# Three places where VectorE stands still in a stack of selective scans: copies of xc moved, an output addition moved, 664 dt x B products given to VectorE

## The chip, the cores and the metric

One core of one Trainium2 chip runs the whole program. The metric is the time of one execution on the device in microseconds, as a median of repeated runs. The profile is of one more execution, and its span runs from the first instruction to the last.

Five engines work side by side, each through its own queue in order: PE (TensorE, matrix products into PSUM), DVE (VectorE), ACT (ScalarE), POOL (GpSimd) and SP (SyncE, which here issues the DMAs).

## The reference, cut to what matters

The input is 8 images of 192 channels and 56 x 56 points. Four layers follow, each a residual on a group norm:

```python
x = x + _L0_conv_ref(_gn(x), ...)
x = x + _L1_conv_ref(_gn(x), ...)
x = x + _L2_conv_ref(_gn(x), ...)
x = x + _L3_conv_ref(_gn(x), ...)
```

Layer 0 applies filters made from each point to 5 x 5 patches; layers 1 to 3 are Mamba layers with an inner width of 512, 384 and 384. The heart of these is the selective scan over the points of an image, with 16 states for each inner channel:

```python
xc = silu(causal_conv(xi) + conv_b)
dbl = xc @ x_proj_W.T
dt = softplus(dt_low_rank @ dt_proj_W.T + dt_proj_b)
h = h * exp(dt[..., None] * A) + (dt * xc)[..., None] * B[:, None, :]
y = einsum('nds,ns->nd', h, C) + xc * D
out = (y * silu(z)) @ out_proj_W.T
```

`dbl` holds the low-rank dt, B and C of 16 each. Layer 1 puts a layer norm before and after, and the three slices of 64 channels share their weights.

## The kernel before, in words

Each image is cut into 7 chunks of T = 448 points; 56 chunks a layer. A **job** is one chunk in layers 2 and 3 (the dense layers, `nd` = 3 groups of 128 inner channels) and one chunk and slice in layer 1 (`nd` = 4, 168 jobs). A job has `nd` x 4 **units**: one group j of 128 channels and one q of four groups of 4 states, so 16 units in layer 1 and 12 in the dense layers; 2688 + 672 + 672 = 4032 in all. A unit lies on 128 partitions (32 channels x 4 states) and has four rows (the 4 times 32 channels), taken in two halves h of two rows.

What a unit k needs, by function, line and engine:

- `decays` (L721, ACT): the exponentials of dt x A for one half, two of them, into a PSUM bank of that half.
- `inputs_lo` (L738, DVE): dt x xc times B for the low half. B was spread over the partitions by a small matmul, `spread_b` (L715, PE), into a PSUM pool with one buffer, `banks.b`. The one for unit k+2 can therefore only begin when DVE has read that of k+1.
- `inputs_hi` (L734, POOL): the same product for the high half, with B out of `rows[0, q]` in SBUF, which a DMA loads (`row_in`, L620).
- `inputs_begin` (L729, ACT): the state at the chunk's start into column 0. `keep` (L746, ACT) saves the last column.
- `scan` (L742, DVE): the recurrence, one instruction for each half.
- `readout` (L751, POOL, twice): the states times C, in place; so it has to wait for `keep` of the same unit. `reduce` (L757, L760, PE) sums over the states, and `gated` (L776, DVE) multiplies a finished group with silu(z).

dt and dt x xc come to the units through memory: `softplus` (L634, ACT) makes dt, `x_again` (L638, PE) copies xc into PSUM, `dtx` (L641, DVE) multiplies the two, `store` sends the group to DRAM (`ops`), and `load_ops` reads it back spread over the partitions (`rep`, two buffers for each half). `load_when_free` issues these loads from SP's queue.

**The order is written out by hand** in `ssm_layer`. The body of unit k issues, in this order: `gated` and `reduce(k-3)`; the plan's place 2m; `scan(k, 0)`; `decays(k+1, 0)`; `inputs_begin(k+3)`; `inputs_hi(k+2)`; two `readout(k-2)`; `inputs_lo(k+1)`; `spread_b(k+2)`; the plan's place 2m+1; `scan(k, 1)`; `keep(k)`; `decays(k+1, 1)`, where m is the unit's number in its job. Idle slots on PE get filler matmuls (`nothing`, L766).

The next job's preparation, and the end of the job before (its output projection and the addition to the stream), are laid into the 2 x `per_job` **places** of a job by `places`. Preparation consists of `Step`s: matmuls, the operation that empties the PSUM bank (`rest`), a cost that spreads the steps over a stretch of places, and `left`: how many emptying operations may still be outstanding when the step begins. `Steps.run` first empties down to `left`, then issues the matmuls. The matmuls' pool `mm` has two buffers. `bounds` says where the stretches begin: the silu block stands at place 8 (dense), 10 (layer 1, first slice) or 6, the softplus block 6 (dense) or 8 places later. A step with `closes` ends its place.

```python
def run(self, steps):
    for step in steps:
        self.flush(step.left)
        ...
            step.matmuls()
            self.pending.append(step.rest)
```

A **block** is where ACT changes its table of functions and back: `silu` (xc at L587, silu(z) of the running job at L568, reload at L560) and `softplus` (L634 and its reload). During a block ACT makes no decays.

In a dense job, `meanwhile` (right behind the silu block) holds the two `out_proj` steps of the job before (L1107, PE) with their additions `add` (L1113, DVE); `xproj` (L592, PE) follows, and then `left_of_b`, `delta` and the row loads. Before the change xproj's step has `left` 1, so that the first addition is issued at place 9, ahead of `scan(k, 1)`.

## Time and profile before

| what | value |
|---|---|
| median of three runs | 26,491.58 us (26,490.21 to 26,491.7) |
| the profiled execution's own time | 26,518.46 us |
| its span | 26,516.6 us |
| mean granted clock of PE | 0.835 |
| POOL busy | 24,242.3 us, 91% of the span |
| DVE busy | 22,849.2 us, 86% |
| PE busy (matmuls) | 22,170.8 us, 84% |
| ACT busy | 17,021.6 us, 64% |

By layer, inside three windows of the trace (layers 1, 2 and 3 without their ends):

| window, us | length | PE | DVE | ACT | POOL | granted clock |
|---|---|---|---|---|---|---|
| 1760 to 17925 | 16165 | 13067 | 14039 | 10852 | 15378 | 0.80 |
| 18240 to 22300 | 4060 | 3519 | 3546 | 2822 | 3824 | 0.87 |
| 22460 to 26400 | 3940 | 3493 | 3421 | 2770 | 3789 | 0.89 |

How to read the profile's lines. A line of the groups gives line, engine, operation, output <- inputs by the program's names with partitions x elements, and the number of instructions; behind the first bar the total busy time and the mean nanoseconds of one; behind the second the idle time of the engine just before them, and what ended most of it. A line of the waits gives who waited <- for whom, then total us, number of waits and the longest. A line of the timeline gives start, length, engine, line, operation and number of equal instructions in a row, and in brackets the idle time ahead and who ended it. Who ended a wait is inferred from semaphores; an engine that isn't the bottleneck may be idle at no cost.

### The profile page before, as it was taken

The page shows a single profiled execution, that of the slowest core. Times are in us where ns is not written, and L with a number is a line of the kernel's source. Part 1 is how long each engine was busy: PE and PEld are TensorE (multiplying, and loading weights), DVE is VectorE, ACT ScalarE, POOL GpSimd, SP SyncE. Part 2 cuts the span into 40 slices and gives each one's busy share as a digit, 9 for nine tenths or more (in the row PEclk, how much of TensorE's full clock was granted, in tenths as well). Part 3 has the DMA queues.
Part 4 walks back from the last instruction along what each step waited for, and adds up shares of the span by engine and source line. Part 5 has one row for each costly group of instructions (what it writes and reads, how often), then busy time and mean ns, then how long its engine had stood idle before and what let it go on. Part 6 is the DMA issues. An engine that isn't in the chain of part 4 may idle for free. (4 is left out here: it accounts for less than half of the span.)

```text
span 26516.6 us, 248987 instructions
## 1 busy us (share of the span) xinstructions
PE 22170.8 (84%) x74628; PEld 7074.0 (27%) x74628; DVE 22849.2 (86%) x17677; ACT 17021.6 (64%) x32354; POOL 24242.3 (91%) x12820
## 2 busy tenths in 40 slices
PE   9988888888888888888878888888888888888888
PEld 3322222222222222222222222222333332333332
DVE  8878888888888888888888888887888887888888
ACT  1146666666666666666666666665666666777776
POOL 4469999999999999999999999998999998999999
PEclk9987878887778787787778877878888888888888
DMA  4433333333333333333333333333344443444443
GB/s 107 110 103 121 119 118 121 119 120 120 119 118 120 120 119 118 120 121 120 117 121 118 121 116 122 119 119 107 131 134 133 134 134 120 134 134 136 140 136 123
DMA packets 1249495, 3236.48 MB, mean 122 GB/s; under 512 B 170924, under 2 KB 510916, under 8 KB 1248008
## 3 DMA queue, kind: packets, MB, share of 16 engines
q1 hardware_dynamic: 1245336, 3219.49, 37.1%
q8 instruction: 585, 9.58, 0.1%
q14 instruction: 774, 6.34, 0.1%
q10 hardware_dynamic: 2800, 1.06, 0.0%
HBM read 2502.68 MB, written 555.55 MB: 115 GB/s over the span
## 5 line engine op out<-in xcount | busy, mean ns | idle before, releaser
L742 DVE TENSOR_TENSOR_SCAN uhg<-da,uhg 128x898 f32<-128x898 f32 x8064 | 16063.3, 2013 | 1003.2 <-ACT da L721 991.9
L751 POOL TENSOR_TENSOR uhg<-uhg,rows 128x896 f32<-128x896 f32 x8064 | 15387.2, 1930 | 809.0 <-ACT carry L746 769.7
L721 ACT ACTIVATE da<-rep,k 128x448 f32<-128x448 f32 x16128 | 10262.0, 636 | 1843.9 <-DVE uhg L742 1531.9
L734 POOL TENSOR_TENSOR uhg<-rep,rows 128x896 f32<-128x896 f32 x4032 | 8407.6, 2085 | 592.2 <-DMA rep<-ops 554.0
L738 DVE TENSOR_TENSOR uhg<-rep,b 128x896 f32<-128x896 f32 x4032 | 4296.4, 1066 | 923.9 <-PE b L715 873.4
L760 PE MATMUL y<-uhg,k 128*32 128x448 f32 x32256 | 4946.3, 658 | 124.0 <-POOL uhg L751 120.6
L746 ACT COPY carry<-uhg 128x4 f32<-128x4 f32 x4032 | 787.6, 195 | 4268.1 <-DVE uhg L742 4259.3
L715 PE MATMUL b<-k,k 96*128 96x448 bf16 x4032 | 1603.6, 398 | 1903.1 <-DVE uhg L738 1895.9
L766 PE MATMUL y<-w_d,k 128*128 128x448 f32 (+1 forms) x5908 | 3015.2, 608 | 0.0
L757 PE MATMUL y<-xc,w_d 128*128 128x448 f32 x2016 | 1411.4, 793 | 835.8 <-DVE zs L776 833.5
L1008 PE MATMUL mm<-xs,k 128*128 128x448 f32 x2688 | 1345.1, 628 | 571.4 <-ACT da L721 413.1
L766 PEld LDWEIGHTS y<-w_d,k 128*128 128x128 f32 x5908 | 1174.3, 220 | 1867.8 <-issue 1841.5
L626 PE MATMUL mm<-dbl,w_dt 36*128 36x448 f32 (+1 forms) x2016 | 1580.7, 897 | 36.1 <-ACT k L608 35.5
L760 PEld LDWEIGHTS y<-uhg,k 128*32 128x32 f32 x32256 | 749.9, 116 | 3182.6 <-issue 1554.8
L1060 PE MATMUL mm<-v,w_in 96*128 96x448 f32 x2688 | 1416.4, 658 | 152.0 <-ACT zs L668 97.7
L431 POOL TENSOR_TENSOR x<-x,one 96x448 f32<-96x448 f32 x560 | 633.2, 1135 | 648.8 <-DVE one L423 631.3
L641 DVE TENSOR_TENSOR dt<-dt,mm 128x448 f32<-128x448 f32 x1008 | 609.1, 618 | 644.5 <-PE mm L638 469.5
L715 PEld LDWEIGHTS <-k 96*128 96x128 bf16 x4032 | 414.7, 103 | 2741.1 <-issue 1641.0
L631 ACT ACTIVATE dt<-mm,k 128x448 f32<-128x448 f32 x1008 | 637.2, 632 | 771.8 <-PE mm L626 761.2
L423 DVE TENSOR_TENSOR prod<-mm,shifted 128x448 f32<-128x448 f32 x1680 | 932.3, 609 | 188.1 <-PE mm L411 167.6
L1087 PE MATMUL mm<-xin,w_conv 128*128 128x448 f32 x2688 | 1076.1, 543 | 0.0
L603 PE MATMUL mm<-dbl,k 16*16 16x448 f32 x1120 | 735.1, 747 | 273.6 <-ACT dbl L596 273.6
(134 smaller groups left out, 20183.0 us busy)
## 6 DMA issues: line engine op xcount, KB each, us to landing
rep<-ops SPq DMA_DIRECT2D x4032, 448.0 KB, 4.7
rows<-bc SPq DMA_DIRECT2D x2240, 224.0 KB, 4.9
ops<-dt SPq DMA_DIRECT2D x1008, 448.0 KB, 2.8
shifted<-xpad SPq DMA_DIRECT2D x672, 179.0 KB, 4.6
xg<-stream SPq DMA_DIRECT2D x168, 336.0 KB, 3.5
xr<-stream SPq DMA_DIRECT2D x168, 336.0 KB, 4.7
stream<-xr SPq DMA_DIRECT2D x112, 336.0 KB, 3.2
xs<-xg SPq DMA_DIRECT2D x224, 112.0 KB, 2.3
```

The costliest lines, as they stand in the source:

```text
L626: nc.tensor.matmul(u.dps[j][:, :T], lhsT=w.dtw[:, j * 128 : (j + 1) * 128], rhs=u.dbl[:nk, :], start=True, stop=True)
L715: nc.tensor.matmul(brow[k][:, :T], lhsT=pick_b[:, q, :], rhs=us[i].parts, start=True, stop=True)
L721: nc.scalar.activation(t[:, 64 + 449 * r : 512 + 449 * r], reps[k // NQ][h][:, r, 0, :], AF.Exp, scale=w.neg_a[:, j * NR + 2 * h + r, q : ...
L734: nc.gpsimd.tensor_mul(uhg[k][:, 2:4, 1:], reps[k // NQ][1][:, :, 1, :], b)
L738: nc.vector.tensor_mul(uhg[k][:, 0:2, 1:], reps[k // NQ][0][:, :, 1, :], b)
L742: nc.vector.tensor_tensor_scan(v, banks.da[h][:, 63:961], v, 0.0, ALU.mult, ALU.add)
L751: nc.gpsimd.tensor_mul(v, v, us[i].rows[1, q].unsqueeze(1).to_broadcast([128, 2, T]))
L757: nc.tensor.matmul(ys[k // NQ][:, :T], lhsT=w.dd[:, j, :], rhs=us[i].xc[:, j, :], start=True, stop=False)
L760: nc.tensor.matmul(y[32 * r : 32 * r + 32, :T], lhsT=fold, rhs=uhg[k][:, r, 1:], start=False, stop=(q == NQ - 1))
L766: nc.tensor.matmul(ys[k // NQ][:, : nd * 112], lhsT=zeros, rhs=w.dd.rearrange("p j e -> p (j e)")[:, : nd * 112], start=False, stop=False,)
L1008: nc.tensor.matmul(pm[:, :T], lhsT=w.inconv[:, k, j * 128 : (j + 1) * 128], rhs=ck.xs[:, i, 2 - 2 * k : 2 - 2 * k + T], start=(k == 0), st ...
L1060: nc.tensor.matmul(pm[:, :T], lhsT=w.inw[:, k, m * 128 : (m + 1) * 128], rhs=ck.v[:, k, :], start=(k == 0), stop=(k == NCT - 1),)
```

## The change

Three things change, all in the order of the work. First, the copies of xc for groups 0 and 1 (`x_again`) are issued at the same place as the softplus block, ahead of `scan(k, 0)`, and not one place later behind `spread_b`; the first `store` step no longer lets one operation be outstanding, so that `dtx(0)` and `dtx(1)` are both issued at place softplus + 2. In the dense jobs `dtx(1)` was one place later. Second, in the dense jobs xproj's step no longer empties anything first: the first output addition is issued at place 10, behind `scan(k, 1)`, by an empty step of cost 3.5 that stands where a pause of that cost stood. Third, a set `by_vector` holds the units behind the silu block and behind the softplus block of each job with a successor and, in the dense layers, the first unit of the next job: 2 x 167 in layer 1 and 3 x 55 in each dense layer, 664 of 4032. For these, `inputs_hi` does nothing and `inputs_lo` makes both halves on DVE, B coming out of PSUM both times. `bounds` and the call of `places` are rewritten so that stretches need not adjoin.

```diff
-        stores[1].closes = True
...
-            + [settle()], [Step(None, silu, 0, 0.3, block=True), *meanwhile] + [Step(xproj, xproj_out, 1, nd)] * (nd == 3),
-            [Step(xproj, xproj_out, 0, nd)] * (nd == 4) + [pause(1.0 if nd == 4 else 3.5)]
+            + [settle()], [Step(None, silu, 0, 0.3, block=True), *meanwhile] + [Step(xproj, xproj_out, 9, nd)] * (nd == 3),
+            ([Step(xproj, xproj_out, 0, nd), pause()] if nd == 4 else [Step(None, lambda: None, 2, 3.5)])
...
-            + [settle()], [Step(None, softplus, 0, 0.3, block=True)],
-            stores[:2] + [Step(None, lambda: store(0), 1)] + stores[2:3] + [Step(None, lambda: store(1), 1)]
+            + [settle()], [Step(None, softplus, 0, 0.3, block=True)] + stores[:2],
+            [Step(None, lambda: store(0), 0)] + stores[2:3] + [Step(None, lambda: store(1), 1)]
...
+        by_vector = set()
+
         def inputs_hi(k):
+            if k in by_vector:
+                return
...
         def inputs_lo(k):
             b = brow[k][:, :T].unsqueeze(1).to_broadcast([128, 2, T])
-            nc.vector.tensor_mul(uhg[k][:, 0:2, 1:], reps[k // NQ][0][:, :, 1, :], b)
+            for h in range(2 if k in by_vector else 1):
+                nc.vector.tensor_mul(uhg[k][:, 2 * h : 2 * h + 2, 1:], reps[k // NQ][h][:, :, 1, :], b)
...
-            return 0, silu, silu + 2, softplus, softplus + 1, softplus + 4, n_places
+            return (0, silu), (silu, silu + 2), (silu + 2, softplus), (softplus, softplus + 1), (softplus + 2, softplus + 4), (softplus + 4, n_places)
...
-                    plan = places(*zip((*jobs[i + 1][2](u, us[i], outs), rest + jobs[i + 1][3](u)), at, at[1:]))
+                    by_vector |= {k + at[1][0] // 2 + 1, k + at[3][0] // 2 + 1} | ({k + per_job} if nd == 3 else set())
+                    stretches = *jobs[i + 1][2](u, us[i], outs), rest + jobs[i + 1][3](u)
+                    plan = places(*((steps, *p) for steps, p in zip(stretches, at)))
```

## The prediction

> **What bounds the kernel now.** I read the engine totals first, then the costliest groups, and then, layer by layer, whom each engine waits for.

> ```profile
> PE 22170.8 (84%) x74628; PEld 7074.0 (27%) x74628; DVE 22849.2 (86%) x17677; ACT 17021.6 (64%) x32354; POOL 24242.3 (91%) x12820
> ...
> L742 DVE TENSOR_TENSOR_SCAN uhg<-da,uhg 128x898 f32<-128x898 f32 x8064 | 16063.3, 2013 | 1003.2 <-ACT da L721 991.9
> L751 POOL TENSOR_TENSOR uhg<-uhg,rows 128x896 f32<-128x896 f32 x8064 | 15387.2, 1930 | 809.0 <-ACT carry L746 769.7
> ...
> L734 POOL TENSOR_TENSOR uhg<-rep,rows 128x896 f32<-128x896 f32 x4032 | 8407.6, 2085 | 592.2 <-DMA rep<-ops 554.0
> L738 DVE TENSOR_TENSOR uhg<-rep,b 128x896 f32<-128x896 f32 x4032 | 4296.4, 1066 | 923.9 <-PE b L715 873.4
> ```

> POOL is the busiest engine, so a change that takes 664 of its products away looks like a large gain. But the right-hand columns show POOL waiting: its readouts (L751) wait for `keep`, which is one step behind DVE's scans, and its product (L734) waits for a DMA. By layer (layer 1, then 2, then 3; total us, times, longest one):

> ```profile
> POOL uhg L751 <- ACT carry L746: 746.2, 637, 3.3
> ```
> ```profile
> POOL uhg L734 <- DMA rep<-ops: 268.2, 51, 71.7
> ```
> ```profile
> POOL uhg L734 <- DMA rep<-ops: 207.7, 53, 62.9
> ```

> The reverse wait, DVE's scan for POOL, comes to almost nothing:

> ```profile
>   ACT da L721: 991.9, 820
>   POOL uhg L751: 4.6, 10
>   POOL uhg L734: 1.0, 4
> ```

> In layer 1, POOL's own pace is 5.81 us a unit (2.04 from one product's start to the next instruction, 3.77 for two readouts), 92.9 us for a job of 16 units, and a job lasts 98.0 us. So the scan chain on DVE leads, stopping at the two table blocks of each job. In layers 2 and 3, 12 x 5.81 = 69.7 us; with 196.5/50 = 3.9 and 144.8/52 = 2.8 us of wait for `rep` (the totals less the first fill, 71.7 and 62.9) that gives 73.6 and 72.5, and the jobs last 73.9 and 72.5. POOL there is full but for one wait a job, and that wait ends when the next job's data, made by DVE, ACT and PE, comes through memory. POOL is nearly tied with the chain, not ahead of it. Only PE waits for it, in layer 3 (layer 2: 16.2 us):

> ```profile
> PE y L760 <- POOL uhg L751: 58.3, 87, 0.9
> ```

> Now the two places where DVE stands still. First the silu block of a layer 3 job (start, length, instruction, in brackets the wait):

> ```profile
> 23325.17 1.28 ACT L587 ACT_TABLE_LOAD   x1
> 23325.77 1.09 DVE L738 TENSOR_TENSOR uhg<-rep,b 128x896 f32<-128x896 f32 x1
> 23327.12 0.36 PE L715 MATMUL b<-k,k 96*128 96x448 bf16 x1
> 23327.32 4.67 PE L1107 MATMUL mm<-zs,w_out 128*96 128x448 f32 x12
> ...
> 23329.78 0.62 DVE L1113 TENSOR_TENSOR xr<-xr,mm 96x448 f32<-96x448 f32 x1 [2.92 <-PE mm L1107]
> 23330.31 1.31 ACT L721 ACTIVATE da<-rep,k 128x448 f32<-128x448 f32 x2
> 23330.32 3.93 DVE L742 TENSOR_TENSOR_SCAN uhg<-da,uhg 128x898 f32<-128x898 f32 x2
> ```

> DVE waits 2.92 us for the output projection (L1107) with a scan behind it whose decays are long there. Then the softplus block of the same job, where DVE stands at both brackets:

> ```profile
> 23347.44 1.28 ACT L634 ACT_TABLE_LOAD   x1
> ...
> 23350.88 0.62 DVE L641 TENSOR_TENSOR dt<-dt,mm 128x448 f32<-128x448 f32 x1 [1.33 <-PE mm L638]
> ...
> 23352.71 2.03 DVE L742 TENSOR_TENSOR_SCAN uhg<-da,uhg 128x898 f32<-128x898 f32 x1 [1.21 <-ACT da L721]
> ...
> 23355.64 1.15 DVE L641 TENSOR_TENSOR dt<-dt,mm 128x448 f32<-128x448 f32 x2
> ```

> [...] The moved product reads one input from PSUM, so I expect no contention; L738's mean of 1066 ns beside a busy POOL agrees. [...] The trace's granted clock is 0.80, 0.87 and 0.89 in layers 1 to 3, with PE 81, 87 and 89% busy, and I come back to this in the range.

> **The change part by part.** It touches 167 jobs of layer 1 and 55 each of layers 2 and 3 (those with a predecessor).

> Products to DVE. Two a job in layer 1 and three in the dense layers: 334 + 330 = 664. POOL loses 664 x 2.04 = 1355 us. DVE gains 664 x 0.98 = 651 us (0.98 from one product's start to the next instruction). At silu, the next decays are ready 7.20 us after L587's load in layer 1 and DVE idles 3.3 to 3.9 us, so 0.98 is hidden: cost 0. At softplus they are ready 5.61 us (layer 1) and 5.24 us (dense) after L634's load, with 2.3 to 3.0 idle: hidden too, even beside both `dtx`. If decays came earlier, each would cost up to 0.98. The first unit of a dense job has no such stall: from 5 us behind softplus to the end of the job DVE runs without a break, so 0.98 x 110 = **+108 us** on the path (between 0, where PE holds the end, and 108; I take 108). DVE's data is there: its low half starts 5.5 to 8.8 us after POOL got the same job's `rep`. POOL no longer meets the DMA at that unit: its next product comes 3.77 us later.

> The longer product holds its PSUM bank 0.98 us longer, and `spread_b(k+2)`, which writes that bank (one buffer), stands on PE ahead of the planned matmuls. At the dense silu that is L1107 and then xproj.

> Addition behind the switch. The scan no longer stands behind L1113 and its 2.92 us; it runs inside the stall. The scan after it starts 0.85 us (layer 2) and 1.21 us (layer 3) later than its decays allow now: mean 1.03 saved. Given back: L1107 starts later by 0.1 to 0.98, middle 0.54. Net -0.49 x 110 = **-54 us** (ends -0.93 and -0.05 a job). Next late is ACT's pair of decays. xproj's bank now waits for an addition of 0.62 us that comes when L1107 ends; behind it on PE stand the matmuls of place 10.

> Copies of xc beside softplus. Both `dtx` now fall into the stall. In the dense layers the second one stood ahead of a scan: 0.54 x 110 = **-59 us** (1.15 for two less the overlap: 0.54 from start to start). In layer 1 both stood there already; what goes is what the copy added to the wait, 0.09 x 167 = -15 us. The stores' DMAs on SP's queue follow `dtx`, a place earlier for the second; SP's row loads keep their order.

> PE's waits for POOL: 58.3 + 16.2 = 74.5 us at most. POOL comes 6 us a job earlier against waits of 0.9, so they go, but not all stood on the path; I take three quarters: **-56 us** (0 to -74.5).

> Layer 1 in sum: -15 as above; the few jobs in which POOL led (it waits for `keep` 637 times, not everywhere), -20 (0 to -40); `spread_b` held back at 334 units, hidden beside the table loads but for some 0.05 each, +15 (0 to 0.4 x 167 = +67). **-20 us**.

> Sum: -54 - 59 + 108 - 56 - 20 = -81 against the profiled execution's 26,518.5 (span 26,516.6): 26,437. It lay 27 above the median of the three runs, so the forecast is **26,410**. A difference of 0.2% (53 us) is about what measurement can tell from none.

> **Rivals.**
> (B) POOL leads in the dense layers. For it: 94 and 96% busy, and POOL's pace plus one wait makes up the job to 0.3 us. Against: its wait ends on the others' data. If its relief carries until DVE (64.4 and 62.8 us busy a job) or PE (64.9) stops it, I estimate half of the 6.1 us: 2.7 x 110 = -300, so 26,190.
> (C) Slower: `spread_b` behind the longer product. It stands ahead of L1107 and xproj on PE, and PE ends last in the dense stretch from silu to softplus as soon as it loses more than the 0.49 of slack that the addition's move gives. Then +0.5 x 110 + 0.4 x 167 = +122: 26,613. PE's clock works the same way: layer 1's triples of jobs last 290, 293.7 or 296.9 us[...].
> (D) Nothing: the next wait (decays behind the reload) swallows each gain, 26,490.
> (E) POOL is the bound all through: -1355, so 25,135. DVE's waits for it, 5.6 us, speak against it.

> **How the numbers follow.** Mine 0.45 (its own range 26,340 to 26,470 from the ends above), B 0.18, C 0.18, D 0.17, E 0.02. Of mine a quarter (0.11) is above 26,439, within 0.2%. Faster 0.34 + 0.18 + 0.02 = 0.54; same 0.11 + 0.17 = 0.28; slower 0.18. The range takes in B's 26,190 and nearly C's middle: 26,180 to 26,600.

> **What would show it.** Right: 3368 instructions on POOL's L734 product; the extra DVE products inside the two stalls, with the next scan starting within 0.1 us of its decays; L1113's wait gone or under 0.7; POOL's wait for `rep`, beyond the first fill, under 60 us a layer; dense jobs about 0.5 us shorter, layer 1's as long as now. A drop of 2 us or more in dense jobs says B; L1107 or xproj ending last, with DVE waiting on L715, says C. The prediction is wrong if layer 1 moves by more than 60 us either way, which would be the clock or POOL.

## The result, and the profile after

The changed kernel takes 26,033.4 us (median of four runs, 26,015.8 to 26,051.6) against 26,490.9 us before: a ratio of 0.9834, 95% interval 0.9819 to 0.9850, or 458 us less. The profiled execution took 26,015.75 us with a span of 26,014.0. The forecast was 26,410, and its range ended at 26,180 below: the direction was right, the size was more than five times too small (81 us in the sum).

The page of the changed kernel, in the rows that answer to those of before (L748 is the scan, L757 the readout, L739 POOL's product, L744 VectorE's, and further down L766 is `reduce`):

```profile
PE 21700.6 (83%) x74628; PEld 7024.6 (27%) x74628; DVE 23443.2 (90%) x18341; ACT 17023.5 (65%) x32354; POOL 22914.3 (88%) x12156
...
L748 DVE TENSOR_TENSOR_SCAN uhg<-da,uhg 128x898 f32<-128x898 f32 x8064 | 16076.1, 2013 | 788.2 <-ACT da L720 786.0
L757 POOL TENSOR_TENSOR uhg<-uhg,rows 128x896 f32<-128x896 f32 x8064 | 15372.3, 1930 | 1559.4 <-ACT carry L752 1542.1
...
L739 POOL TENSOR_TENSOR uhg<-rep,rows 128x896 f32<-128x896 f32 x3368 | 7019.7, 2084 | 652.7 <-DMA rows<-bc 392.8
L744 DVE TENSOR_TENSOR uhg<-rep,b 128x896 f32<-128x896 f32 x4696 | 4954.1, 1066 | 750.6 <-PE b L714 687.2
```

The 664 products have moved at the price expected (1066 ns on VectorE each), and POOL lost 1328 us of work. But POOL's idle time grew too: its wait for `keep` doubled. One thing is unexplained by this table: TensorE has exactly as many matmuls as before (74,628) and yet 470 us less busy time. Keep that in mind.

POOL's waits in layer 3 (total us, times, longest), and TensorE's for POOL in the whole kernel (120.6 us before):

```profile
POOL uhg L739 <- DMA rows<-bc: 189.0, 47, 6.3
...
POOL uhg L739 <- DMA rep<-ops: 67.7, 2, 64.1
```
```profile
PE y L766 <- POOL uhg L757: 34.4, 47, 1.2
```

The wait for `rep` is down to the first fill, as expected; a wait for the row loads has come in its place, about 4 us a job, which POOL now can afford.

The time by layer is worked out from the trace: from one start of the silu block's table load to the next is a job. S is that load, S' the softplus block's.

| | layer 1 job | layer 2 job | layer 3 job | S to S', layers 2 and 3 | at half clock (granted 0.50) between S+12 and S+24, layers 2 and 3 |
|---|---|---|---|---|---|
| before | 97.71 | 73.90 | 72.46 | 22.40, 22.74 | 9.89, 9.80 us |
| after | 96.09 | 72.22 | 69.87 | 19.74, 19.52 | 3.71, 3.28 us |

Layer 1 gave 1.6 us in each of 168 jobs (some 270 us, where I had 20), the dense layers 1.7 and 2.6. In the dense layers the stretch from S to S' lost 2.7 and 3.2 us and the rest of the job gained 1.0 and 0.6. The last column is the clue: TensorE ran at half clock for 10 us of this stretch before, and for 3.5 after.

The silu block of a layer 3 job of the changed kernel:

```profile
23294.65 1.28 ACT L587 ACT_TABLE_LOAD   x1
...
23295.26 2.08 DVE L744 TENSOR_TENSOR uhg<-rep,b 128x896 f32<-128x896 f32 x2
...
23297.26 2.02 DVE L748 TENSOR_TENSOR_SCAN uhg<-da,uhg 128x898 f32<-128x898 f32 x1
23297.40 0.36 PE L714 MATMUL b<-k,k 96*128 96x448 bf16 x1 [0.72 <-DVE uhg L744]
23297.60 4.67 PE L1115 MATMUL mm<-zs,w_out 128*96 128x448 f32 x12
...
23299.79 1.31 ACT L720 ACTIVATE da<-rep,k 128x448 f32<-128x448 f32 x2
23300.05 0.62 DVE L1121 TENSOR_TENSOR xr<-xr,mm 96x448 f32<-96x448 f32 x1 [0.78 <-PE mm L1115]
...
23301.13 2.03 DVE L748 TENSOR_TENSOR_SCAN uhg<-da,uhg 128x898 f32<-128x898 f32 x1 [0.47 <-ACT da L720]
```

Both products and a scan fit into the stall, and the next scan starts 0.03 us after its decays (23299.79 + 1.31 = 23301.10). It starts at S + 6.49 in both dense layers, as a median; before it started at S + 7.09 in layer 2 and 7.75 in layer 3. The output projection begins at S + 2.95 in both; before at S + 2.16 and 2.82. So it is 0.79 us later in layer 2 and 0.13 in layer 3, 0.46 on average, inside the 0.1 to 0.98 that I had given.

Now what that one microsecond does further on. TensorE in the job of before, from about S + 10:

```profile
23335.29 0.36 PE L715 MATMUL b<-k,k 96*128 96x448 bf16 x1
23336.19 0.92 PE L603 MATMUL mm<-dbl,k 16*16 16x448 f32 x2 [0.54 <-ACT dbl L596]
23336.95 0.35 PE L604 MATMUL mm<-k,k 16*16 16x448 bf16 x1
23337.23 1.02 PE L626 MATMUL mm<-dbl,w_dt 44*128 44x448 f32 x2
23338.17 1.29 PE L760 MATMUL y<-uhg,k 128*32 128x448 f32 x8
23339.74 1.86 PE L626 MATMUL mm<-dbl,w_dt 44*128 44x448 f32 x2 [0.27 <-ACT k L608]
23341.53 1.67 PE L603 MATMUL mm<-dbl,k 16*16 16x448 f32 x2
```

It waits 0.54 us for ACT's copy of dbl (L596). Some 3 us later the same two matmuls L626 take 1.86 instead of 1.02 us. The windows view of before says why (stretch, length, busy us of PE, PEld, DVE, ACT and POOL with counts, granted clock, DMA share, GB/s):

```profile
23336.00:23339.00 3.00, 2.81 (x13) 0.64 (x13) 3.00 (x2) 1.79 (x5) 3.00 (x2) 0.94 0.08 19
23339.00:23348.00 9.00, 8.73 (x18) 2.06 (x18) 7.64 (x7) 6.19 (x13) 9.00 (x6) 0.50 0.10 27
```

The deltas, which softplus waits for, run at clock 0.50 for 9 us, while PE counts as 97% busy. After, the same places of the job:

```profile
23305.60:23308.60 3.00, 3.00 (x14) 0.64 (x13) 3.00 (x3) 1.93 (x5) 3.00 (x2) 1.00 0.22 42
23308.60:23314.10 5.50, 5.50 (x18) 1.58 (x18) 5.50 (x5) 4.91 (x10) 5.50 (x4) 0.80 0.09 29
```

dbl's copy comes at S + 10.04 instead of S + 11.11 (medians of layer 3), TensorE has no hole there, and the clock stays up until the deltas are through: 3.1 us from the second delta's start to the last one's end (S + 14.00 to 17.10) instead of 5.7 (15.24 to 20.95). In layer 2 the copy comes 0.41 us earlier, and the same stretch goes from 5.7 us (14.57 to 20.29) to 3.1 as well. But look at the second line: TensorE is busy all through these 5.50 us, and its clock is 0.80. It fell, at the end of the deltas, without a hole. What makes it fall is taken up again behind the experiments.

### The profile page after: what moved, and what is told of

The parts are those of the page before. It is cut to its first block, busy times and chain, and to the rows that moved or that the text cites. A ratio compares the mean times of both kernels' runs of the same rounds, so it can differ in the third digit from the quotient of the medians.

```text
span 26014.0 us, 248999 instructions
## 1 busy us (share of the span) xinstructions
PE 21700.6 (83%) x74628; PEld 7024.6 (27%) x74628; DVE 23443.2 (90%) x18341; ACT 17023.5 (65%) x32354; POOL 22914.3 (88%) x12156
## 5 line engine op out<-in xcount | busy, mean ns | idle before, releaser
L748 DVE TENSOR_TENSOR_SCAN uhg<-da,uhg 128x898 f32<-128x898 f32 x8064 | 16076.1, 2013 | 788.2 <-ACT da L720 786.0
L757 POOL TENSOR_TENSOR uhg<-uhg,rows 128x896 f32<-128x896 f32 x8064 | 15372.3, 1930 | 1559.4 <-ACT carry L752 1542.1
L739 POOL TENSOR_TENSOR uhg<-rep,rows 128x896 f32<-128x896 f32 x3368 | 7019.7, 2084 | 652.7 <-DMA rows<-bc 392.8
L744 DVE TENSOR_TENSOR uhg<-rep,b 128x896 f32<-128x896 f32 x4696 | 4954.1, 1066 | 750.6 <-PE b L714 687.2
L766 PE MATMUL y<-uhg,k 128*32 128x448 f32 x32256 | 4771.9, 659 | 34.6 <-POOL uhg L757 34.4
L752 ACT COPY carry<-uhg 128x4 f32<-128x4 f32 x4032 | 786.8, 195 | 4095.2 <-DVE uhg L748 4082.0
L772 PE MATMUL y<-w_d,k 128*128 128x448 f32 (+1 forms) x5908 | 2911.9, 589 | 0.0
L1068 PE MATMUL mm<-v,w_in 96*128 96x448 f32 x2688 | 1492.6, 689 | 362.1 <-ACT zs L667 191.9
L766 PEld LDWEIGHTS y<-uhg,k 128*32 128x32 f32 x32256 | 716.1, 116 | 2874.5 <-issue 1742.5
L626 PE MATMUL mm<-dbl,w_dt 36*128 36x448 f32 (+1 forms) x2016 | 1283.7, 742 | 0.0
L638 PE MATMUL mm<-xc,k 128*128 128x448 f32 x2016 | 1026.1, 621 | 13.7 <-DVE dt L641 13.7
L1068 PEld LDWEIGHTS mm<-v,w_in 96*128 96x128 f32 x2688 | 595.2, 237 | 1502.7 <-issue 786.2
L1030 PE MATMUL mm<-xs,k 64*128 64x448 f32 x1344 | 895.8, 764 | 62.2 <-ACT zs L665 61.1
```

The source lines that it names most:

```text
L626: nc.tensor.matmul(u.dps[j][:, :T], lhsT=w.dtw[:, j * 128 : (j + 1) * 128], rhs=u.dbl[:nk, :], start=True, stop=True)
L739: nc.gpsimd.tensor_mul(uhg[k][:, 2:4, 1:], reps[k // NQ][1][:, :, 1, :], b)
L744: nc.vector.tensor_mul(uhg[k][:, 2 * h : 2 * h + 2, 1:], reps[k // NQ][h][:, :, 1, :], b)
L748: nc.vector.tensor_tensor_scan(v, banks.da[h][:, 63:961], v, 0.0, ALU.mult, ALU.add)
L757: nc.gpsimd.tensor_mul(v, v, us[i].rows[1, q].unsqueeze(1).to_broadcast([128, 2, T]))
L766: nc.tensor.matmul(y[32 * r : 32 * r + 32, :T], lhsT=fold, rhs=uhg[k][:, r, 1:], start=False, stop=(q == NQ - 1))
```

## The experiments

All times are medians beside runs of the kernel before on the same chip (26,468 to 26,495 us); the ratio's 95% interval is in brackets. Jobs are the means of layers 1, 2 and 3.

**One part at a time.** In `copies_only`, `addition_only` and `products_only` the other two parts are put back as they were. My theory after the result (A in the expectations) was order and clock in the dense layers and POOL's relief in layer 1; the rival (B) was POOL's relief everywhere.

The edits, cut, against the changed kernel, in this order: no products; no addition; no copies (with the stretch behind softplus and `closes` as before, too); no first unit (for `no_first_unit`).

```diff
-                    by_vector |= {k + at[1][0] // 2 + 1, k + at[3][0] // 2 + 1} | ({k + per_job} if nd == 3 else set())
+                    by_vector |= set()
...
-... [Step(xproj, xproj_out, 9, nd)] * (nd == 3),
-            (... else [Step(None, lambda: None, 2, 3.5)])
+... [Step(xproj, xproj_out, 1, nd)] * (nd == 3),
+            (... else [pause(3.5)])
...
-            + [settle()], [Step(None, softplus, 0, 0.3, block=True)] + stores[:2],
-            [Step(None, lambda: store(0), 0)] + ...
+            + [settle()], [Step(None, softplus, 0, 0.3, block=True)],
+            stores[:2] + [Step(None, lambda: store(0), 1)] + ...
...
-                    by_vector |= {k + at[1][0] // 2 + 1, k + at[3][0] // 2 + 1} | ({k + per_job} if nd == 3 else set())
+                    by_vector |= {k + at[1][0] // 2 + 1, k + at[3][0] // 2 + 1}
```

> Only the copies of xc beside softplus, with both dtx in the stall; products and addition as before. Theory A (the addition's move and TensorE's half-clock window between silu and softplus made the dense gain, POOL's relief the gain of layer 1): dense jobs 0.3 to 0.6 us shorter, layer 1 within 30 us, so 26,400 to 26,470. Theory B (POOL's relief made nearly all of the gain): within 30 us of before, since POOL's work is unchanged, 26,460 to 26,500.

Measured: 26,347.7 us, 0.9947 (0.9932 to 0.9962); jobs 97.13, 72.97, 71.74. The dense layers gain 0.9 and 0.7 us a job, somewhat more than the 0.54 worked out, and layer 1 gains 0.6, which neither theory had. The gain of the dense layers lies behind S': S to S' stays within 0.15 us of before.

> Only the output addition behind the silu switch. Theory A: the stretch from silu to softplus is 2 to 3 us shorter in dense jobs unless POOL's pace of 69.7 us a job stops it, layer 1 unchanged: 26,180 to 26,330. Theory B: POOL is full in the dense layers and keeps its pace, the stretch shortens by under 0.5 us a job: 26,430 to 26,490.

Measured: 26,241.1 us, 0.9905 (0.9888 to 0.9921); jobs 97.60, 71.95, 69.74; S to S' 20.18 and 19.81. The time lies where theory A put it, in the dense layers alone. The addition alone gives 240 us, of which I had foreseen 54. And layer 3's job is now 69.74 us, which is POOL's pace, 12 x 5.81 = 69.72.

> Only VectorE's 664 products. Theory A: layer 1 about 270 us shorter, dense jobs 0 to 0.5 us longer each: 26,220 to 26,300. Theory B: nearly the whole gain, 26,030 to 26,120, with the stretch from silu to softplus 2 us or more shorter in dense jobs.

Measured: 26,552.5 us, 1.0025 (1.0017 to 1.0034): slower. Layer 1 is 1.35 us a job shorter (96.36), the dense jobs 2.5 and 2.4 us longer (76.37, 74.83). So relieving POOL without shortening the chain is a loss in the dense layers, where theory B expected the gain. Theory A missed too: it had these jobs at most 0.5 us longer. Some 1.8 and 2.2 us of the loss lie behind S', and no run takes them apart.

> The changed kernel with POOL making the first unit's product of dense jobs again (two products a job on VectorE everywhere). Theory A: that product stood in VectorE's unbroken stretch, so dense jobs are up to 0.98 us shorter without it: 25,930 to 26,030. Theory B: POOL has 2.04 us a job more and waits for the repeated dt again, dense jobs 1 to 2 us longer: 26,140 to 26,250.

Measured: 25,856.0 us, 0.9763 (0.9748 to 0.9777): 177 us better than the whole change and beyond both theories' ranges, on A's side; jobs 96.12, 70.14, 68.82. The first unit's product costs 1.05 us a job in layer 3, as VectorE's time says, and 2.1 in layer 2.

**Is it POOL's relief?** `copies_addition` has no product on VectorE (`by_vector |= set()` in the changed kernel). `pool_again` has the two products in the stalls, but POOL still makes them too, into a spare tile that nobody reads:

```diff
-            nc.gpsimd.tensor_mul(uhg[k][:, 2:4, 1:], reps[k // NQ][1][:, :, 1, :], b)
+            nc.gpsimd.tensor_mul(spare if k in by_vector else uhg[k][:, 2:4, 1:], reps[k // NQ][1][:, :, 1, :], b)
```

> The copies and the addition as changed, no product on VectorE. If the two gains are independent (134 and 240 us in the runs that had one of them alone), 26,480 - 374 = 26,110. If POOL's pace of 12 x 5.81 = 69.7 us a job now stops the dense layers (the run with the addition alone had layer 3 jobs of 69.74 us), 26,150 or more, with layer 3 jobs at 69.7 and POOL's waits in the dense layers near zero.

Measured: 26,146.9 us, 0.9862 (0.9847 to 0.9876); jobs 97.04, 71.96, 69.73. Layer 3 stands at POOL's pace, layer 2 is 2.2 us above it. In layer 3 TensorE now waits for POOL much more than the 58.3 us of before, and POOL for `rep` hardly at all:

```profile
PE y L766 <- POOL uhg L757: 259.2, 370, 1.3
```
```profile
POOL uhg L739 <- DMA rep<-ops: 6.0, 3, 3.0
```

> The kernel without the first unit's product (two products a job on VectorE), but POOL still makes each of those products too, into a spare tile that nobody reads, so that POOL is relieved of nothing. If POOL's relief is what the products bring, the time falls back to that of the kernel with no products or worse, 26,100 to 26,250, layer 1 jobs at 97 us. If the gain is in where the product lies (the unit's data ready earlier, fewer waits for the row loads), it stays near 25,860, up to 25,930.

Measured: 25,974.9 us, 0.9793 (0.9777 to 0.9810); jobs 96.17, 71.18, 69.63. The answer differs by layer. In layer 3 the relief is what counts: with POOL's work given back it stays at POOL's pace, and TensorE's wait is the same as without products (261.2 us; 72.4 in `no_first_unit`). In layer 2 the relief is 1.0 of the products' 1.8 us a job (71.96, 71.18, 70.14 without products, with POOL's work given back, and with the relief); the other 0.8 come without it. Layer 1 keeps its whole gain, 96.17 against 96.12, although POOL is relieved of nothing. So there my theory falls: the gain is not POOL's.

**Is it the clock, in the dense layers?** Fillers (L766) added to the kernel before, with nothing else touched (the last two lines in `before_filled` alone):

```diff
+            if nd == 3 and m == 5:
+                nothing(k - 3, 2)
             bg.run(plan[2 * m + 1])
+            if nd == 3 and m == 5:
+                nothing(k - 3, 3)
```

> The kernel before with five more filler matmuls in the sixth unit of each dense job (two ahead of the plan's second place, three behind it), where TensorE stood still for some 0.5 us and its clock fell to half for the deltas behind. Nothing else is moved. If the clock carries part of the addition's gain, the half-clock time between silu and softplus goes and the stretch is 1 to 1.8 us shorter: 26,290 to 26,380. If the gain was the order alone, the fillers are in the way: 26,480 to 26,540.

Measured: 26,462.3 us, 0.9989 (0.9980 to 0.9997); jobs 97.70, 73.41, 72.06. The half-clock time ahead of softplus went, but S to S' fell only to 21.8 and 21.9: the three fillers behind the plan's place stand ahead of the second delta, which began at S + 16.3 instead of 15.2. The expected size was missed, through the experiment's own fillers.

> The kernel before with only the two fillers ahead of the plan's second place in the sixth unit of each dense job, none behind it (those had pushed the second delta 1.1 us back). If the clock carries about half of the addition's gain, half-clock time between silu and softplus stays away and the stretch is 1.3 to 2 us shorter than before: dense jobs 71.5 to 72.5 us in layer 2, 70.5 to 71.3 in layer 3, 26,280 to 26,400. If the second hole in TensorE's work, before the second delta, suffices to lose the clock, no change: 26,460 to 26,510.

Measured, without those three: 26,283.2 us, 0.9929 (0.9914 to 0.9944); jobs 97.55, 72.02, 70.17; S to S' 20.03 and 20.52. Two useless matmuls a job give 189 us, with nothing else moved: that the clock carries this time is shown. TensorE and the clock in such a job:

```profile
23343.84 1.29 PE L766 MATMUL y<-w_d,k 128*128 128x336 f32 x4
23345.07 0.92 PE L603 MATMUL mm<-dbl,k 16*16 16x448 f32 x2
...
23346.10 1.02 PE L626 MATMUL mm<-dbl,w_dt 44*128 44x448 f32 x2
23347.05 0.96 PE L760 MATMUL y<-uhg,k 128*32 128x448 f32 x8
23348.09 1.02 PE L626 MATMUL mm<-dbl,w_dt 44*128 44x448 f32 x2
23349.03 0.92 PE L603 MATMUL mm<-dbl,k 16*16 16x448 f32 x2
```
```profile
23344.50:23347.50 3.00, 3.00 (x16) 0.74 (x14) 3.00 (x2) 1.78 (x4) 3.00 (x2) 1.00 0.12 26
23347.50:23353.50 6.00, 5.92 (x27) 1.54 (x20) 6.00 (x6) 5.40 (x11) 6.00 (x4) 1.00 0.14 35
```

The fillers lie in the hole that L603 had waited through; the second L626 takes 1.02 us, not 1.86, and the clock is 1.00.

**What is it in layer 1?** `silu_product` has VectorE's product behind the silu block alone. `silu_rows` is the same with B for the high half out of SBUF, so that the PSUM bank is free as early as before (the second part of the diff; `first_rows`, below, does it for the first unit alone).

```diff
-                    by_vector |= {k + at[1][0] // 2 + 1, k + at[3][0] // 2 + 1} | (...)
+                    by_vector |= {k + at[1][0] // 2 + 1}
...
+                    b = us[i].rows[0, q].unsqueeze(1).to_broadcast([128, 2, T])
+                nc.vector.tensor_mul(uhg[k][:, 2:4, 1:], reps[k // NQ][1][:, :, 1, :], b)
```

> The copies and the addition as changed, with VectorE's product behind the silu block alone. If each of the two products gives POOL's 2.04 us the same worth, half of the way from the kernel with no products to the one with two: about 26,000, layer 1 jobs 96.6 us. If POOL's lateness matters only where TensorE then feeds the softplus block, nearly all of it is the silu product's: 25,870 to 25,930.

Measured: 25,848.5 us, 0.9746 (0.9732 to 0.9761); jobs 96.18, 70.52, 68.25. It is as good as `no_first_unit` with its two products a job, and it has all of their gain in layer 1: what counts lies behind the silu block.

> The kernel with VectorE's product behind the silu block alone, with B for that product's high half out of SBUF (the row that POOL used) and not out of the PSUM bank. POOL's relief, VectorE's work and its order stay; only the bank is free 1 us earlier, and the next spread of B on TensorE with it. If layer 1 gained because TensorE's work was held back 1 us and so reached nearer to the deltas (clock), layer 1 jobs return to about 97.0 us and the whole to about 25,990. If the relief or the order of VectorE was the reason, 25,830 to 25,880 and 96.2 us.

Measured: 27,293.8 us, 1.0311 (1.0293 to 1.0328); jobs 98.59, 78.94, 78.81. Neither expectation: the product itself became the bound (in this kernel L748 is the product out of SBUF, L752 the scan, L761 the readout).

```profile
L748 DVE TENSOR_TENSOR uhg<-rep,rows 128x896 f32<-128x896 f32 x277 | 1864.7, 6732 | 0.0
```
```profile
27081.34 3.81 POOL L761 TENSOR_TENSOR uhg<-uhg,rows 128x896 f32<-128x896 f32 x2
...
27083.14 10.79 DVE L748 TENSOR_TENSOR uhg<-rep,rows 128x896 f32<-128x896 f32 x1
27085.12 2.07 POOL L739 TENSOR_TENSOR uhg<-rep,rows 128x896 f32<-128x896 f32 x1
27087.15 3.80 POOL L761 TENSOR_TENSOR uhg<-uhg,rows 128x896 f32<-128x896 f32 x2
27090.91 2.07 POOL L739 TENSOR_TENSOR uhg<-rep,rows 128x896 f32<-128x896 f32 x1
27093.85 2.01 DVE L752 TENSOR_TENSOR_SCAN uhg<-da,uhg 128x898 f32<-128x898 f32 x1
```

The same 128 x 896 product takes 1.07 us with one input in PSUM and here 10.79: it ends at 27093.93, 0.95 us after POOL's own run has ended (27090.91 + 2.07 = 27092.98) and POOL waits. The layers' totals say nothing on the bank, then. But in two of layer 1's three kinds of jobs (by the slice that is being prepared, the first and the third) most of these products took about 2 us, short enough for the stall, so that the next scan starts at S + 7.23 as in `silu_product`. There S to S' is 27.5 and 27.7 us, as with no product (27.7, 27.8), and not 26.3 and 26.4 as in `silu_product`. POOL is relieved there and VectorE's order is the new one, but the bank isn't held, and the gain is gone. This speaks for the bank, but not cleanly: the second slice's jobs in between were 5 us longer than in `silu_product`.

`layer1_filled` is `copies_addition` with fillers ahead of `spread_b` behind the silu block:

```diff
+            if nd == 4 and i + 1 < len(jobs) and m == bounds(jobs[i + 1])[1][0] // 2:
+                nothing(k - 3, 3)
             if k + 2 < n_units:
                 spread_b(k + 2)
```

> The copies and the addition as changed, no product on VectorE; in layer 1 three filler matmuls (some 1.1 us at full clock) ahead of the spread of B behind the silu block, so that TensorE's work there ends 1.1 us later, as the longer product makes it. If layer 1's gain from the products came by TensorE's clock, layer 1 jobs go from 97.0 to about 96.2 us and the whole from 26,147 to about 26,010. If it came by POOL's relief or VectorE's order, or if later work on TensorE is only late, 26,140 to 26,200.

Measured: 25,901.7 us, 0.9778 (0.9761 to 0.9794), 245 us less than `copies_addition`; jobs 95.63, 71.68, 69.62. Three fillers do in layer 1 as much as the product does, and more. Half-clock time between S+10 and S+27, where the deltas are: 10.7 us a job in `copies_addition`, 10.5 in `silu_rows`, 8.7 in `silu_product`, 8.8 in `pool_again`, 9.1 here. The product held `spread_b` and all of TensorE's work behind it 1 us back (in the first slice's jobs xproj ends at S + 10.9 instead of 9.9, while dbl's copy stays at S + 13.55 either way), so there TensorE had 1 us less to stand still ahead of the deltas.

The two gains aren't the same in every part, though. With the product the half-clock time is moved, not removed: from S to S+10 it grows from 1.8 us a job to 3.6 (`silu_product`), and over a whole job it stays (38.4 us without products, 38.7 with); the fillers bring it to 35.3. And of the fillers' 1.4 us a job only 0.8 lie between S and S', where all of the product's 0.9 lie. That the product's gain in layer 1 comes from TensorE's later work is supported by these runs; that the clock is all of it is not shown.

**The first unit.**

> The changed kernel with B for the high half of the first unit of each dense job out of SBUF instead of the bank. If that unit's product costs by the time it takes in VectorE's unbroken stretch (0.98 us), the time stays within 40 us of the changed kernel's: 25,990 to 26,070. If it costs by holding the bank, and so TensorE, most of the 177 us comes back: 25,860 to 25,920.

Measured: 26,119.2 us, 0.9871 (0.9856 to 0.9885), some 90 us more than the changed kernel and in neither range; jobs 96.11, 72.27, 71.35. In layer 2 the job is as in the changed kernel, with a product of 1.2 us on average: holding the bank isn't the price there. In layer 3, where all of the excess is (1.5 us a job), the product took 1.9 us on average, so this run doesn't answer for that layer. All of these products (least, median, most: 1079, 1430, 3002 ns):

```profile
L748 DVE TENSOR_TENSOR uhg<-rep,rows x110: 1079/1430/3002, 18030.5 to 26022.2; 128x896 f32<-128x896 f32 x110
```

**Do the causes add up?** The kernel before with both sets of fillers and nothing of the change; and copies and addition, layer 1 filled, with VectorE's product behind the silu block in the dense jobs alone. The first has the diffs of `before_filled_2` and `layer1_filled`, the second that of `layer1_filled` and this, against the changed kernel:

```diff
-                    by_vector |= {k + at[1][0] // 2 + 1, k + at[3][0] // 2 + 1} | ({k + per_job} if nd == 3 else set())
+                    by_vector |= {k + at[1][0] // 2 + 1} if nd == 3 else set()
```

> The kernel before with fillers alone: two in each dense job, three in each job of layer 1, nothing moved. If the change's gain is TensorE's clock, the two gains add (189 and 245 us): 26,040 to 26,090, about the time of the changed kernel. If part of the change's gain is of another kind, the fillers stop short of it, at 26,150 or more.

Measured: 26,053.8 us, 0.9848 (0.9834 to 0.9863); jobs 96.08, 72.22, 70.53. Fillers alone, none of the change: within 21 us of the changed kernel, whose ratio is 0.9834. The 414 us are nearly the sum of the two (434). That they equal the change's 458 so closely is in part chance: the change also holds the copies' gain (134 us alone) and the first unit's loss (177), which the fillers don't touch.

> Copies and addition as changed, fillers in layer 1 and no product there, VectorE's product behind the silu block in the dense jobs alone. If clock and relief are two gains, layer 1 jobs at 95.6 us and dense jobs at 70.5 and 68.3: 25,740 to 25,790. If the relief was only another way to keep the clock, no better than 25,850 to 25,900.

Measured: 25,767.7 us, 0.9740 (0.9723 to 0.9758); jobs 95.62, 70.43, 68.29. It is the best kernel of this study, 266 us under the changed one. The two gains add; but one lies in layer 1 and the other in the dense layers, so the run doesn't say how they add within a layer.

## Why the prediction was wrong, point by point

- **POOL is not the bound before**: right. Products alone made the kernel slower by 71 us, rival E is excluded. But I stopped there. 69.7 us a job was a floor just under the dense jobs' 72 to 74, and once the chain is shorter it decides in layer 3: 69.73 with copies and addition, 68.8 with the relief. Relief and shorter chain had to be costed together. `no_first_unit` against `pool_again`: 119 us.
- **"PE's waits for POOL: 58.3 + 16.2 = 74.5 us at most"**: the bound was wrong for this reason. Without the products the waits grow to 259 us in layer 3 alone when the chain shortens; in the changed kernel they are 2.0 us there. So what the products take away is more than the waits of before.
- **The addition, -54**: measured -240. The step that failed is "Next late is ACT's pair of decays", behind the net of -0.49: I followed the saved microsecond to there and no further, and put the time of TensorE's work behind it as fixed. The terms of the net were near. The give-back ("middle 0.54") was 0.46 on average in the changed kernel, and ACT's copy of dbl came 0.41 us (layer 2) and 1.07 us (layer 3) earlier, 0.74 for 0.49. But TensorE waits for this copy, and where its work fell changed the clock of the deltas: from the second one's start on they took 2.6 us less in both layers, a term that the prediction didn't have. Earlier order is 0.6 us (second delta at S + 14.00, not 14.57) and 1.2 us (not 15.24). How order and clock share the job's gain exactly stays open, since fillers alone gave 1.9 and 2.3 us a job. L1113's wait, which was to go under 0.7 us, went from 3.27 to 0.79 on average.
- **Layer 1, -20**: measured about -270, past the 60 us that the prediction had named as its sign of "the clock or POOL". 0.7 us a job are there with copies and addition, 0.95 more with the products. For these, "`spread_b` held back ... +15" had the wrong sign. In rival C the late `spread_b` was the price; here it went with the gain: in the first slice's jobs TensorE stood still 1 us more ahead of `spread_b` and 1 us less ahead of the deltas.
- **The clock** stood in the prediction only as a risk, in rival C and in what would prove it wrong. The records to cost it were there: in every dense job of before it fell to 0.50 between S + 8 and S'. I read its mean by layer (0.87, 0.89) and not by place in a job.
- **First unit's product, +108**: measured +177. Right in layer 3 (1.05 us for 0.98). In layer 2 it cost 1.1 us more than VectorE's time. The half-clock time of a job is 4.4 us longer with it there (16.7 against 12.3), but it is 4.2 us longer in layer 3 too, where nothing more was lost, so this alone doesn't explain it: it stays open.
- **Products in the stalls at cost 0**: right, scans start 0.03 us after their decays behind both blocks, in all three layers (medians).
- **Copies, -74**: measured -134 alone. Direction and place were right in the dense layers; 0.6 us a job in layer 1, where I had 0.09, came unforeseen, and no run here took it apart.
- **A slip in rival B**: half of 6.1 us is 3.05, not 2.7, which makes it 26,155. It changes nothing above.

**What makes the clock fall.** In all sixteen kernels, all changes of the granted clock, between 1.00 and 0.50, lie within 0.04 us of a grid of 3413.3 ns. A hole much shorter than one step of this grid went with a fall: in the job of before it was 0.54 us, a sixth of a step, and fillers in it kept the clock (`before_filled_2`). But the hole isn't the cause by itself. Cut along this grid, these are the window of the job of before that has the hole, and two windows of the changed kernel, one behind the other:

```profile
23335.23:23338.65 3.42, 2.86 (x18) 0.74 (x14) 3.42 (x3) 2.21 (x7) 3.42 (x3) 1.00 0.07 17
```
```profile
23308.42:23311.83 3.41, 3.41 (x12) 0.88 (x8) 3.41 (x4) 2.88 (x7) 3.41 (x3) 1.00 0.19 56
23311.83:23315.25 3.42, 3.42 (x11) 0.70 (x10) 3.42 (x4) 3.34 (x6) 3.42 (x3) 0.50 0.00 0
```

TensorE is busy for all of the second window (3.41 of 3.41 us), and the clock falls from 1.00 to 0.50 behind it all the same. What the first two have in common is matmuls with few rows in use (the first number of `16*16` and `44*128`). If the time of each matmul counts by its rows out of 128, the first window comes to 0.34 and the second to 0.39; the window with the two fillers (23343.55 to 23346.96) comes to 0.55, and the clock stays. This holds throughout. In the dense layers of the sixteen traces, 30,868 windows ran at full clock (granted 1.00). The clock fell behind 3,846 of them; all of these have a share by rows under 0.50, and all the others have one above 0.40. One boundary at 0.45 sorts 98.6% of them, while the plain busy time sorts 95.2% at best and was 95% or more ahead of 688 falls. In layer 1 it is 98.6% of 45,627 windows (boundary 0.46), against 92.5%. From half clock (0.50) the full clock came back behind no window with a share under 0.75. This is read out of traces, since no run changed the rows alone. It fits the fillers, which use all 128 rows; whether fillers of few rows would do less was not run.

## What to carry to other kernels

Look at TensorE's granted clock by place in the repeated job, not as a mean: here a chain with matmuls of 16 and 44 rows lost the clock (granted 0.50), with a stop of 0.54 us in the kernel before and with none in the changed one. In the former two matmuls of it took 1.86 us and not 1.02, while TensorE counted as 97% busy. Before crediting a change that moves work, run the old kernel with fillers at that place (here 0.9848 without any of the change, beside the change's 0.9834), and compare by layer: what they give alone is not due to the new order. And when a chain is shortened, ask which engine's plain pace lies next below: here POOL's relief was worth something only then, and in the unbroken stretch of VectorE the moved product cost 1 to 2 us a job.
